# Stage 1 from six products instead of seven, its blocks evicted by ScalarE and summed by GpSimd, with side work moved to the end of a turn

## The chip, the core and the metric

The kernel runs on one core of a Trainium2 chip. The metric is device time in microseconds for one execution. The engines are TensorE (PE in the profile, with its weight loads as PEld), VectorE (DVE), ScalarE (ACT), GpSimd (POOL) and SyncE (SP), which issues nearly all DMAs. All data are fp32.

## The reference

A residual block is computed over x of shape 128 x 64 x 1024 (samples, channels, length): four one-dimensional convolutions with three taps and 64 channels, whose weights are modulated per sample by a style vector and demodulated.

```python
s = style @ mw.T + mb
weight = SCALE * w * s[:, None, :, None]
demod = lax.rsqrt(jnp.sum(weight * weight, axis=(2, 3)) + EPS)
weight = weight * demod[:, :, None, None]
...
TYPES = ('same', 'upsample', 'same', 'downsample')
...
x = x + _L0_cond_ref(x, cond_512, weights, biases, mod_w, mod_b)
```

`upsample` is a transposed convolution followed by a blur, `downsample` a blur followed by a convolution of stride two. There is no nonlinearity between the layers. So, away from the ends of a row, the four layers are for each sample one convolution of 64 x 64 matrices, and that is how the kernel treats them.

## The kernel before

The 128 samples are taken four at a time: 32 groups, numbered q. For each group the combined taps are built out of the layers' weights in three chained stages of small matmuls, and then x is convolved with them.

**Weights of a group.** `scale3(q)` (ScalarE) makes `wd`, the scaled weights of the last layer. **Stage 1** multiplies them with the third layer's weights: two kernels of three taps give one of five, the blocks S0 to S4 of 64 columns, kept in the tile S (eight slots of 64 columns for each of two row halves). From group 3 on (`DIRECT`), all but group 6 of these are computed in two parts, `stage1_a` and `stage1_b`, which work from sums of taps (`w3x`, `w2n`, made once by `split_weights`): seven products of 64 columns in five groups of matmuls. The first part leaves products in the PSUM tile psS, ScalarE evicts them with a factor `tBn`, and the second part goes on accumulating into the same PSUM; VectorE then evicts the two mixed blocks, and GpSimd makes one sum (L484). **Stage 2** (PSUM psR) convolves S with the blur E. For groups 8 to 30 two of its sums are shared: `share_sums` (VectorE) adds blocks of S, `share` multiplies them one turn ahead into spare columns of psA, and `share_copy` (ScalarE) copies them into psR as its starting values: the seeds. The evicted result is R; `r_sums` adds two more blocks to it. **Stage 3** (`stage3_b`, `stage3_a`) gives the taps Wf, and `combine_a` and `combine_b` (VectorE) make the tiles H from them.

psS, psR and psW are three uses of the same two PSUM buffers (pool `ps_w`, one buffer for each of its two tags). So the seeds of stage 2, or its first matmul where there are none, wait for the last eviction of psS.

**The convolution** is in Toom-Cook form: from the input planes X, VectorE makes G (`in_g01` and `in_g2`, at L712), and from G and X the five tiles T0 to T4 (`in3`, `in04` on VectorE; `in1`, `in2` on GpSimd, L776 and L781). Five products `conv0` to `conv4` (L803) of 340 columns go to psA, or for `conv4` to the one PSUM tile Y, which `sum2` (VectorE, two instructions) fills with starting values just before.

**Order.** Everything is issued in an order written out by hand; each engine runs its own list in that order and waits on semaphores. Groups 0 to 3 are done in `early_turn`, the middle ones in `turn_of(q)` (which works on q, n = q+1, c = q+2 and s = q+4 at once; q = 4 is called the entry), the last three in code of their own. TensorE's order in a middle turn is: stage 2 of c, `conv2(q)`, `stage3_b(c)`, `conv4(q)`, `stage3_a(c)`, `conv3(n)`, `stage1_a(s)`, `conv0(q)`, `stage1_b(s)`, `share(c+1)`, `conv1(n)`. In four turns (`SLOTS`: 10, 14, 15, 19) a further set of matmuls for the ends of the rows stands before `conv1(n)`. `SIDE` is a table by q of small work on VectorE, for those ends and for later groups: one to four short instructions in 21 turns besides the entry's own.

**Lines that matter below.** L428: matmuls of stage 1. L399: ScalarE's scaled evictions (S, R, Wf) and wd. L484: GpSimd's sum in S. L481: VectorE's eviction of stage 1. L506 and L589: matmuls of stage 2. L638: `r_sums`. L712: every multiply-add of VectorE (G, H, `sum1`, `sum2`). L761: `in3`. L790: `in04`. L803: convolutions. L880: outputs.

Of the kernel before, what the change touches and what calls it, by code (L numbers as in the profile page):

```python
# [63 lines left out]
def kernel(  # L64
# [339 lines left out]
    w3x = const.tile([P, 5, C], F32, name="w3x")  # L404
    w2n = const.tile([P, 5, C], F32, name="w2n")

    def split_weights():
        nc_g.tensor_copy(w3x[:, :K], w3)
        nc_g.tensor_scalar_mul(w2n[:, :K], woi[2], -1.0)
        for t, src in ((w3x, w3), (w2n, woi[2])):  # L410
            nc_g.tensor_add(t[:, K:], src[:, : K - 1], src[:, 1:])
# [3 lines left out]
    def scale3(q, engs=(nc_a, nc_a)):  # L415
        wd = []
        src = w3 if q < DIRECT else w3x
        n = src.shape[1]
        for j in range(2):
            t = wd_pool.tile([P, 5, C], F32, tag="wd", name=f"wd{q}_{j}")  # L420
            scaled_copy(engs[j], t[:, :n], src, tA[:, q, j : j + 1])
            wd.append(t)
        chain[q] = wd
# [17 lines left out]
    def flat(t):  # L441
        return t.rearrange("c a o -> c (a o)")
# [3 lines left out]
    def stage1(q, pool=None, engs=(nc_a, nc_a), between=None):  # L446

        wd = chain[q]
        ps = unit(pool or ps_w, f"psS{q}")
        for k, (at, at1) in enumerate(((0, 3), (3, 1), (1, 4))):  # L450
            tap_matmul(ps, wd, at, 2, woi[2][:, k, :], EVEN, first=k == 0)
            tap_matmul(ps, wd, at1, 1, woi[2][:, k, :], slice(1, 2), last=k == K - 1)
        if between:
            between()
        st, _ = s_tiles(q)
        for r in range(2):
            scaled_copy(engs[r], flat(st[r][:, 1:6]), ps[r][:, : 5 * C], tB[:, q, r : r + 1])
        chain[q] = st
        return ps

    def stage1_a(q, ps=None):

        ps = ps or unit(ps_w, f"psS{q}")
        wd = chain[q]
        tap_matmul(ps, wd, 2, 2, w2n[:, 0, :], EVEN, first=True)
        tap_matmul(ps, wd, 3, 2, w2n[:, 2, :], EVEN)
        tap_matmul(ps, wd, 1, 1, w2n[:, 1, :], slice(1, 2))
        st, t = s_tiles(q)
        for r in range(2):
            scaled_copy(nc_a, flat(st[r][:, :4]), ps[r][:, C : 5 * C], tBn[:, q, r : r + 1])  # L470
        chain[q] = wd, ps, st, t

    def stage1_b(q):

        wd, ps, st, t = chain[q]
        tap_matmul(ps, wd, 2, 1, w2n[:, 3, :], slice(3, 4))
        tap_matmul(ps, wd, 4, 1, w2n[:, 4, :], slice(4, 5), last=True)
        for r in range(2):
            p1 = st[r][:, 0:1, :].to_broadcast([P, 2, C])
            sums = ps[r][:, 2 * C : 6 * C].rearrange("c (a b o) -> c a b o", a=2, b=2)[:, :, 0]  # L480
            nc_v.scalar_tensor_tensor(  # L481
                st[r][:, 4:6, :], sums, tB[:, q, r : r + 1], p1, op0=ALU.mult, op1=ALU.subtract
            )
        nc_g.tensor_add(t[:, :, 2], t[:, :, 2], t[:, :, 0])  # L484
        chain[q] = st
        whole[q] = t
# [12 lines left out]
    def share_sums(q):  # L499
        t = whole[q]  # L500
        nc_v.tensor_add(t[:, :, 6:8], t[:, :, 1:5:3], t[:, :, 2:6:3])
# [13 lines left out]
    def share(q, ps):  # L515

        at = [NB + 4 + i * C for i in range(3)]
        p12, p34 = ([b[:, i:j] for b in ps] for i, j in zip(at, at[1:]))
        chain_matmul(p12, E[:, 2], chain[q], slice(6, 7))
        chain_matmul(p34, E[:, 6], chain[q], slice(6, 7))  # L520
        chain_matmul(p34, E[:, 5], chain[q], slice(7, 8), True)
        shared_ps[q] = [b[:, at[0] : at[2]] for b in ps]
# [12 lines left out]
    def stage2_rest(q):  # L535
# [5 lines left out]
            (apart, E[:, 0], slice(1, 4, 2)),  # L541
            (block(1), Ed[:, 0], slice(2, 3)),
            (block(2), Ed[:, 1], slice(1, 2)),
            (block(3), E[:, 2], slice(3, 4)),
            (block(3), Ed[:, 2], slice(2, 3)),
            (block(4), Ed[:, 3], slice(1, 2)),
            (block(4), E[:, 4], slice(3, 4)),
            (block(5, 2), E[:, 8], slice(2, 4)),
            (block(5), E[:, 6], slice(3, 4)),
            (block(1, 2), E[:, 1], slice(4, 6)),  # L550
            (block(2), E[:, 3], slice(4, 5)),
            (block(3), Ed[:, 4], slice(5, 6)),
            (block(4), Ed[:, 5], slice(4, 5)),
            (block(5), E[:, 7], slice(5, 6)),
# [22 lines left out]
    def stage2_taps(q, taps, ps):  # L577

        st = chain[q]
        for n in taps:  # L580
            e = n - 2
            if e % 2 == 0:
                a, lo, m = slice(1, 4), e // 2 + 1, 3
            else:
                a, lo, m = slice(4, 6), (e + 3) // 2, 2
# [897 lines left out]
    def turn_of(q):  # L1483
        n, c, s = q + 1, q + 2, q + 4
        entry = q == FIRST
        stage2(c)
        if entry:
# [33 lines left out]
        side(SIDE, q)  # L1521
# [30 lines left out]
        if s + 1 < NQ:  # L1552
            scale3(s + 1)
# [168 lines left out]
```

## Time and profile before

| what | us |
|---|---|
| median of 3 runs (lowest, highest) | 475.72 (475.56, 475.97) |
| span of the profiled execution | 475.5 |
| granted TensorE clock, mean | 0.998 |
| ScalarE busy | 312.0 |
| GpSimd busy | 165.8 |
| 28 calls of in1, of in2 on GpSimd, mean | 1.652, 1.660 |
| 31 calls of in04 on VectorE, mean | 1.585 |
| HBM traffic over the span | 145 GB/s |

The span runs from the first to the last instruction; the runs lie 0.06 to 0.47 us above it. In a row of the timeline stand the start, the time to the end of the last of the xN instructions merged in it, engine and line, what is written from what, the shape, and in brackets the idle time before it and what ended that. Two numbers after a group's bar are its busy time in us and the mean of one in ns. The start of an instruction that waits for a shared resource, not for a semaphore, is the start of its wait, so its time contains that wait. TensorE's ends are modelled; the start of the next group is the better guide to when it was done.

### The profile page before, as it was taken

What the parts mean: (1) busy time and instruction counts of PE and PEld (TensorE: products, weight loads), DVE (VectorE), ACT (ScalarE), POOL (GpSimd) and SP (SyncE); (2) the same over time, 40 slices, a digit from 0 to 9 for tenths busy, and PEclk for the clock granted to TensorE, in tenths of its full rate; (3) what the DMA queues carried; (4) which work ended last, traced back from release to release, by engine and by line L of the source; (5) the groups of instructions that cost most, each with busy time, mean ns of one, the idle gap of its engine ahead of it and who ended that gap; (6) DMA issues with size and microseconds to landing.
All of it is one profiled execution on the core that took longest, in us unless ns stands there. A gap on an engine that the chain in (4) does not pass through costs nothing.

```text
span 475.5 us, 26771 instructions
## 1 busy us (share of the span) xinstructions
PE 469.7 (99%) x11932; PEld 349.5 (74%) x11932; DVE 417.3 (88%) x694; ACT 312.0 (66%) x711; POOL 165.8 (35%) x200
## 2 busy tenths in 40 slices
PE   9999999999999999999999999999999999999996
PEld 6987788777678876677776677766788787876653
DVE  3889998879989998899979899979998999999896
ACT  4565657577766676766667666667666777766464
POOL 3634033664444342233432233422333423243200
PEclk9999999999999999999999999999999999999999
DMA  5237456535445554345544454543555544455225
GB/s 176 71 115 224 150 151 180 152 113 177 139 145 166 166 166 136 123 150 169 163 150 126 130 168 152 178 124 121 152 164 169 164 145 147 148 152 161 80 91 193
DMA packets 52707, 70.71 MB, mean 149 GB/s; under 512 B 6000, under 2 KB 50672, under 8 KB 52592
## 3 DMA queue, kind: packets, MB, share of 16 engines
q1 hardware_dynamic: 52368, 68.78, 46.3%
q8 instruction: 93, 1.52, 1.4%
q10 hardware_dynamic: 224, 0.22, 0.1%
q14 instruction: 22, 0.18, 0.1%
HBM read 35.36 MB, written 33.62 MB: 145 GB/s over the span
## 4 chain that ended last, share of the span: by engine, by line
PE 99%; DVE 0%; ACT 0%; issue 0%
PE psA L803 47%; PE Y L803 12%; PE psR L506 9%; PE psW L621 7%; PE psA L621 7%; PE psS L428 6%; PE psR L589 5%; PE psA L506 2%; PE Y L1044 2%; PE Y L183 1%; PE Y L379 1%; PE psM L220 0%; PE psE L1044 0%; PE Y L255 0%; DVE o L882 0%; PE psM L255 0%
## 5 line engine op out<-in xcount | busy, mean ns | idle before, releaser
L803 PE MATMUL psA<-T,H 64*64 64x340 f32 x2304 | 185.9, 446 | 0.0
L803 PEld LDWEIGHTS psA<-T,H 64*64 64x64 f32 x2304 | 90.7, 133 | 46.9 <-issue 2.5
L712 DVE SCALAR_TENSOR_TENSOR G<-X 128x1376 f32<-128x1376 f32 (+2 forms) x65 | 78.0, 1206 | 0.2
L776 POOL TENSOR_TENSOR T<-G 128x684 f32<-128x684 f32 x28 | 46.3, 1652 | 73.7 <-DVE G L712 73.7
L484 POOL TENSOR_TENSOR S<-S 128x128 f32<-128x128 f32 x28 | 21.6, 772 | 139.7 <-ACT S L399 139.6
L399 ACT ACTIVATE R<-psR,tC 128x448 f32<-128x448 f32 x63 | 36.6, 631 | 43.6 <-PE psR L506 25.8
L803 PE MATMUL psA<-T,Wf 64*64 64x340 f32 x768 | 63.7, 446 | 0.0
L803 PE MATMUL Y<-T,Wf 64*64 64x340 f32 x768 | 62.4, 451 | 0.0
L712 DVE SCALAR_TENSOR_TENSOR Y<-m,psA 128x340 f32<-128x340 f32 x62 | 32.0, 516 | 28.2 <-PE psA L803 26.9
L399 ACT ACTIVATE psW<-psA 128x128 f32<-128x128 f32 x100 | 19.3, 268 | 49.1 <-PE psA L621 45.0
L790 DVE TENSOR_TENSOR T<-G 128x1368 f32<-128x1368 f32 (+1 forms) x33 | 50.8, 1541 | 0.0
L399 ACT ACTIVATE Wf<-psW,t 128x256 f32<-128x256 f32 (+2 forms) x76 | 32.7, 480 | 26.7 <-PE psW L621 26.4
L761 DVE TENSOR_TENSOR T<-X 128x684 f32<-128x684 f32 x32 | 47.7, 1492 | 0.0
L506 PE MATMUL psR<-S,E 64*64 64x64 f32 (+1 forms) x1472 | 46.8, 237 | 0.0
L781 POOL TENSOR_TENSOR T<-G 128x684 f32<-128x684 f32 x28 | 46.5, 1660 | 0.0
L428 PEld LDWEIGHTS psS<-wd,w2n 64*64 64x64 f32 x1120 | 35.1, 133 | 12.9 <-issue 0.3
L506 PEld LDWEIGHTS psR<-S,E 64*64 64x64 f32 x1472 | 39.5, 134 | 4.9 <-ACT psR L529 0.2
L803 PEld LDWEIGHTS Y<-T,Wf 64*64 64x64 f32 x768 | 30.3, 132 | 16.8
L803 PEld LDWEIGHTS psA<-T,Wf 64*64 64x64 f32 x768 | 29.8, 133 | 14.5
L880 ACT ACTIVATE o<-psA,tb,td 128x340 f32<-128x340 f32 x63 | 37.1, 648 | 5.0 <-PE psA L803 2.8
L880 ACT ACTIVATE o<-y,tb,td 128x340 f32<-128x340 f32 x62 | 38.5, 678 | 0.0
L880 ACT ACTIVATE o<-Y,tb,td 128x340 f32<-128x340 f32 x62 | 36.1, 639 | 2.8 <-PE Y L803 2.0
(180 smaller groups left out, 840.4 us busy)
## 6 DMA issues: line engine op xcount, KB each, us to landing
out<-o SPq DMA_DIRECT2D x191, 170.0 KB, 2.6
X<-in_x SPq DMA_DIRECT2D x150, 172.0 KB, 3.4
X<-in_x SPq DMA_DIRECT2D x14, 516.0 KB, 5.0
par<-in_params SPq DMA_DIRECT2D x3, 192.0 KB, 3.8
Xe<-in_x_ends SPq DMA_DIRECT2D x1, 512.0 KB, 4.5
out<-Oe SPq DMA_DIRECT2D x2, 96.0 KB, 2.1
out<-o ACTq DMA_DIRECT2D x1, 170.0 KB, 2.8
par<-in_params SPq DMA_DIRECT2D x1, 160.0 KB, 2.7
```

The costliest lines, as they stand in the source:

```text
L399: nc_a.activation(dst, src, AF.Copy, scale=f)
L428: nc.tensor.matmul(ps[r][cols, at * C : (at + n) * C], weight[rows], wd[c if r == 0 else 1 - c][rows, taps], start=first, stop=last, skip_ ...
L506: nc.tensor.matmul(dst[r][cols], weight[rows], st[c if r == 0 else 1 - c][rows, slots, :], start=False, stop=last, skip_group_check=True,)
L589: nc.tensor.matmul(ps[r][cols, lo * C : (lo + m) * C], E[rows, e + 2, :], src[rows, a, :], start=(n == 0), stop=(n == 8), skip_group_check ...
L621: nc.tensor.matmul(dst[r][cols], weight[rows], t[rows, c, slots, :], start=first, stop=last, skip_group_check=True,)
L712: nc_v.scalar_tensor_tensor(out, x, f, y, op0=ALU.mult, op1=op)
L761: nc_v.tensor_sub(t[:, pairs, 0, :NJ], plane(X, 3, pairs), plane(X, 1, pairs))
L776: eng.tensor_add(t[:, :, 0, :NJ], plane(g, 2), plane(g, 1))
L781: eng.tensor_sub(t[:, :, 1, :NJ], plane(g, 2), plane(g, 1))
L790: nc_v.tensor_sub(t[:, pairs, :, :NJ], both(a, PL), both(b, 1))
L803: nc.tensor.matmul(ps[s][cols, :NB], w, Ts[q, tag][rows, c, i, g : g + NB], start=(g == 0 and (m == 3 or alone)), stop=(g == K - 1), skip_ ...
L880: nc_a.activation(dst, src, AF.Identity, bias=add, scale=d3)
```

## The change

Stage 1 of the split groups is written with six products of one block each: three in `stage1_a`, three in `stage1_b`, each group of matmuls 64 columns wide. ScalarE evicts everything: in the first part two instructions per half in place of one (two blocks into slots 0 and 4, one into slot 6), in the second one of three blocks per half, which VectorE had done. GpSimd makes S1, S2 and S3 final with four instructions in place of one (L472, L473, L484, L485 of the new file). `w3x`, `w2n` and `wd` have six blocks instead of five, so `scale3` copies 384 columns instead of 320. S0 to S4 lie in slots 0 to 4; the slot numbers in stage 2 follow. In `stage1` of groups 0, 1, 2 and 6 the same nine products are issued as three groups of 192 columns instead of six of 128 and 64.

In the middle turns `scale3(s)` moves from the end of the turn before to behind stage 2; `in_g01` follows `in_g2` directly; the seeds (`share`, `share_copy`) stand ahead of the outputs `outputs(q, 1)` and `outputs(q, 0)`; and the side work of turn q+1 is issued at the end of turn q, behind `in3` and `in1`.

```diff
-        tap_matmul(ps, wd, 2, 2, w2n[:, 0, :], EVEN, first=True)
-        tap_matmul(ps, wd, 3, 2, w2n[:, 2, :], EVEN)
-        tap_matmul(ps, wd, 1, 1, w2n[:, 1, :], slice(1, 2))
+        for n, (i, at) in enumerate(((0, 1), (2, 3), (1, 4))):
+            tap_matmul(ps, wd, at, 1, w2n[:, i, :], slice(i, i + 1), first=n == 0)
         st, t = s_tiles(q)
         for r in range(2):
-            scaled_copy(nc_a, flat(st[r][:, :4]), ps[r][:, C : 5 * C], tBn[:, q, r : r + 1])
+            src = ps[r][:, C : 5 * C].rearrange("c (a b o) -> c a b o", a=2, b=2)[:, :, 0]
+            scaled_copy(nc_a, st[r][:, 0:5:4, :], src, tBn[:, q, r : r + 1])
+            scaled_copy(nc_a, st[r][:, 6], ps[r][:, 4 * C : 5 * C], tBn[:, q, r : r + 1])
+        nc_g.tensor_add(t[:, :, 7], t[:, :, 0], t[:, :, 4])
+        nc_g.tensor_sub(t[:, :, 7], t[:, :, 7], t[:, :, 6])
...
-        tap_matmul(ps, wd, 2, 1, w2n[:, 3, :], slice(3, 4))
-        tap_matmul(ps, wd, 4, 1, w2n[:, 4, :], slice(4, 5), last=True)
+        for n, (i, at) in enumerate(((3, 1), (4, 3), (5, 2))):
+            tap_matmul(ps, wd, at, 1, w2n[:, i, :], slice(i, i + 1), last=n == K - 1)
         for r in range(2):
-            p1 = st[r][:, 0:1, :].to_broadcast([P, 2, C])
-            sums = ps[r][:, 2 * C : 6 * C].rearrange("c (a b o) -> c a b o", a=2, b=2)[:, :, 0]
-            nc_v.scalar_tensor_tensor(
-                st[r][:, 4:6, :], sums, tB[:, q, r : r + 1], p1, op0=ALU.mult, op1=ALU.subtract
-            )
-        nc_g.tensor_add(t[:, :, 2], t[:, :, 2], t[:, :, 0])
+            src = ps[r][:, C : 4 * C].rearrange("c (a o) -> c a o", o=C)
+            scaled_copy(nc_a, st[r][:, 1:4, :], src, tB[:, q, r : r + 1])
+        nc_g.tensor_sub(t[:, :, 2], t[:, :, 2], t[:, :, 7])
+        nc_g.tensor_sub(
+            t[:, :, 1:4:2], t[:, :, 1:4:2], t[:, :, 6:7].to_broadcast([P, 2, 2, C])
+        )
...
         in_g2(c)
-        side(SIDE, q)
+        in_g01(c)
+        if entry:
+            side(SIDE, q)
+        conv0(q, *((2,) if entry else range(K)))
+        if entry:
+            conv1(n, 0, 1)
+        if s < NQ:
+            stage1_b(s)
         if q in SMALL:
             l, bs = SMALL[q]
             nc_v.memset(high(bs.stop - bs.start), 0.0)
-        conv0(q, *((2,) if entry else range(K)))
-        if entry:
-            conv1(n, 0, 1)
-        outputs(q, 1)
-        if s < NQ:
-            stage1_b(s)
-        in_g01(c)
         if sharing(q):
             share(c + 1, banks(q))
             share_copy(c + 1)
+        outputs(q, 1)
         outputs(q, 0)
...
         in1(c, nc_g)
-        if s + 1 < NQ:
-            scale3(s + 1)
+        side(SIDE, q + 1)
```

Three places show how the instructions moved. The first is VectorE's list at the end of turn 12, from `in04` on: G, S and X are the tiles above, y is `sum1`, T `in3`, Y `sum2`, and Ye and g belong to side work. Before:

```order
L790 TENSOR_TENSOR T_13_3996<-G_3729 128x4x342
L501 TENSOR_TENSOR S_3721<-S_3721 128x2x128
L712 SCALAR_TENSOR_TENSOR G_3999<-X_105 128x2x342
L1066 TENSOR_TENSOR Ye_161<-Ye_161,c_156 128x64x6
L481 SCALAR_TENSOR_TENSOR S_3991<-psS_0_3977,tB,S_3991 128x128
L481 SCALAR_TENSOR_TENSOR S_3991<-psS_1_3978,tB,S_3991 128x128
L712 SCALAR_TENSOR_TENSOR G_3999<-X_105 128x2x688
L712 SCALAR_TENSOR_TENSOR y_13_4062<-psA_3884,m_13_3994 128x680
L761 TENSOR_TENSOR T_14_4064<-X_105 128x2x342
L712 SCALAR_TENSOR_TENSOR Y<-m_13_3994,psA_3884 128x340 x2
```

and with the change:

```order
L793 TENSOR_TENSOR T_13_4063<-G_3787 128x4x342
L504 TENSOR_TENSOR S_3775<-S_3775 128x2x128
L715 SCALAR_TENSOR_TENSOR G_4066<-X_105 128x2x342
L715 SCALAR_TENSOR_TENSOR G_4066<-X_105 128x2x688
L715 SCALAR_TENSOR_TENSOR y_13_4133<-psA_3947,m_13_4061 128x680
L764 TENSOR_TENSOR T_14_4135<-X_105 128x2x342
L1019 SCALAR_TENSOR_TENSOR g_159<-par,g_159 128x192 x2
L715 SCALAR_TENSOR_TENSOR Y<-m_13_4061,psA_3947 128x340 x2
```

The eviction of stage 1 has left VectorE, the two parts of G are neighbours, and the side work (here that of turn 13) stands between `in3` and `sum2`.

The second is GpSimd's list over a middle turn and the start of the next (S: sums of stage 1; T: `in1`, then `in2`; R: `r_sums`). Before:

```order
L484 TENSOR_TENSOR S_5104<-S_5104 128x2x64
L776 TENSOR_TENSOR T_18_5179<-G_5112 128x2x342
L638 TENSOR_TENSOR R_5241<-R_5241 128x2x128
L781 TENSOR_TENSOR T_18_5179<-G_5112 128x2x342
L484 TENSOR_TENSOR S_5374<-S_5374 128x2x64
```

and with the change:

```order
L472 TENSOR_TENSOR S_4334<-S_4334 128x2x64
L473 TENSOR_TENSOR S_4334<-S_4334 128x2x64
L484 TENSOR_TENSOR S_4334<-S_4334 128x2x64
L485 TENSOR_TENSOR S_4334<-S_4334 128x2x2x64
L779 TENSOR_TENSOR T_15_4419<-G_4346 128x2x342
L641 TENSOR_TENSOR R_4477<-R_4477 128x2x128
L784 TENSOR_TENSOR T_15_4419<-G_4346 128x2x342
```

Three more instructions on S stand ahead of `in1`; the first two follow ScalarE's first eviction, the last two its second.

The third is GpSimd's list in the first early turn, where S of group 3 is made (t, td and Da are small tables for later groups). Before:

```order
L335 TENSOR_TENSOR tC<-dm 64x8 x2
L934 TENSOR_TENSOR c0f<-dm,par_s 128x16
L484 TENSOR_TENSOR S_842<-S_842 128x2x64
L335 TENSOR_TENSOR t_136<-dm,var 64x8 x2
L332 TENSOR_SCALAR td<-dm 64x8 x2
L930 TENSOR_TENSOR Da<-sc,dm 128x16
```

and with the change:

```order
L335 TENSOR_TENSOR tC<-dm 64x8 x2
L937 TENSOR_TENSOR c0f<-dm,par_s 128x16
L472 TENSOR_TENSOR S_808<-S_808 128x2x64
L473 TENSOR_TENSOR S_808<-S_808 128x2x64
L484 TENSOR_TENSOR S_808<-S_808 128x2x64
L485 TENSOR_TENSOR S_808<-S_808 128x2x2x64
L335 TENSOR_TENSOR t_136<-dm,var 64x8 x2
L332 TENSOR_SCALAR td<-dm 64x8 x2
```

S of group 3 is read by stage 2 at the start of the next early turn. Its even taps read S0, S2 and S4, its odd taps S1 and S3; they follow GpSimd's third and fourth instruction where they followed ScalarE's and VectorE's evictions and GpSimd's one sum.

More of the change, by code (lines that the diff above doesn't have):

```diff
@@ L401, in scaled_copy @@
             eng.tensor_scalar(dst, src, f, None, op0=ALU.mult)
-    w3x = const.tile([P, 5, C], F32, name="w3x")
-    w2n = const.tile([P, 5, C], F32, name="w2n")
+    w3x = const.tile([P, 6, C], F32, name="w3x")
+    w2n = const.tile([P, 6, C], F32, name="w2n")
     def split_weights():
@@ L449, in stage1 @@
         ps = unit(pool or ps_w, f"psS{q}")
-        for k, (at, at1) in enumerate(((0, 3), (3, 1), (1, 4))):
-            tap_matmul(ps, wd, at, 2, woi[2][:, k, :], EVEN, first=k == 0)
-            tap_matmul(ps, wd, at1, 1, woi[2][:, k, :], slice(1, 2), last=k == K - 1)
+        for k in range(K):
+            tap_matmul(ps, wd, k, K, woi[2][:, k, :], slice(0, K), first=k == 0, last=k == K - 1)
         if between:
@@ L518, in share @@
         p12, p34 = ([b[:, i:j] for b in ps] for i, j in zip(at, at[1:]))
-        chain_matmul(p12, E[:, 2], chain[q], slice(6, 7))
-        chain_matmul(p34, E[:, 6], chain[q], slice(6, 7))
-        chain_matmul(p34, E[:, 5], chain[q], slice(7, 8), True)
+        chain_matmul(p12, E[:, 2], chain[q], slice(5, 6))
+        chain_matmul(p34, E[:, 6], chain[q], slice(5, 6))
+        chain_matmul(p34, E[:, 5], chain[q], slice(6, 7), True)
         shared_ps[q] = [b[:, at[0] : at[2]] for b in ps]
@@ L1486, in turn_of @@
         stage2(c)
+        if s < NQ and not entry:
+            scale3(s)
         if entry:
```

37 lines of the change are left out of this document (19 added, 18 removed).

## The prediction

> **What bounds the kernel now.** I read the busy line and the chain of waits of the page first, then the timeline of one middle turn (turn 12) engine by engine.
>
> ```profile
> PE 469.7 (99%) x11932; PEld 349.5 (74%) x11932; DVE 417.3 (88%) x694; ACT 312.0 (66%) x711; POOL 165.8 (35%) x200
> PE 99%; DVE 0%; ACT 0%; issue 0%
> 215.10 0.40 PE L506 MATMUL psR<-S,E 64*64 64x128 f32 x8
> 228.94 0.40 PE L506 MATMUL psR<-S,E 64*64 64x128 f32 x8
> ```
>
> TensorE is the bound. A middle turn, from one stage 2 to the next, is 228.94 − 215.10 = 13.84 us of matmuls without gaps. So work taken from TensorE is gained in full, and any new wait of TensorE is lost in full. There is one place where such a wait is very near:
>
> ```profile
> 204.91 0.94 PE L621 MATMUL psA<-R,w0s 64*64 64x192 f32 x24
> 206.28 1.95 PE L803 MATMUL Y<-T,Wf 64*64 64x340 f32 x24
> 205.16 1.07 DVE L712 SCALAR_TENSOR_TENSOR Y<-m,psA 128x340 f32<-128x340 f32 x2 [0.97 <-PE psA L803]
> ```
>
> conv2 ends where stage3_b begins (204.91), `sum2` starts 0.25 later, ends at 206.23, and conv4 starts 0.05 behind it. Stage3_b covers this chain with nothing to spare. VectorE came to `sum2` 0.97 us early; whatever uses up more than that stops TensorE.
>
> **Saved on TensorE.** Groups of matmuls start one behind the other, so starts give the price.
>
> ```profile
> 210.53 0.73 PE L428 MATMUL psS<-wd,w2n 64*64 64x128 f32 x24
> 211.08 1.90 PE L803 MATMUL psA<-T,Wf 64*64 64x340 f32 x24
> 212.80 0.41 PE L428 MATMUL psS<-wd,w2n 64*64 64x64 f32 x16
> 213.03 0.53 PE L506 MATMUL psA<-S,E 64*64 64x64 f32 x24
> ```
>
> Stage 1 takes 211.08 − 210.53 = 0.55 and 213.03 − 212.80 = 0.23, together 0.78. Two groups of eight at 64 columns take 0.23, so one takes 0.115. Six of them: 0.69, or 0.68 with 0.114. Saved: 0.10 per split group; GpSimd's sum L484 stands once in each, and there are 28 (row below). **−2.8 us.** The direct groups issue the same columns in fewer instructions: nothing taken, up to −0.2.
>
> **The price of the sums: VectorE and GpSimd share something.** GpSimd's single sum has very different durations for one shape:
>
> ```profile
> L484 POOL TENSOR_TENSOR S<-S x28: 455/821/1622, 40.6 to 426.5; 128x128 f32<-128x128 f32 x28
> 142.56 1.58 DVE L712 SCALAR_TENSOR_TENSOR G<-X 128x1376 f32<-128x1376 f32 x1
> 142.83 1.62 POOL L484 TENSOR_TENSOR S<-S 128x128 f32<-128x128 f32 x1
> 215.42 0.87 DVE L712 SCALAR_TENSOR_TENSOR y<-psA,m 128x680 f32<-128x680 f32 x1
> 215.64 1.65 POOL L776 TENSOR_TENSOR T<-G 128x684 f32<-128x684 f32 x1 [2.61 <-DVE G L712]
> 216.21 1.81 DVE L761 TENSOR_TENSOR T<-X 128x684 f32<-128x684 f32 x1
> ```
>
> The 0.455 us sum, begun under VectorE's G, ended at 144.45, 0.31 after G's end at 144.14. The other way round, `in3`, begun under `in1`, ended at 218.02, 0.73 after `in1` (217.29). So two such instructions exclude each other from start to end; who holds it first finishes, the waiting one goes next and then needs about 0.14 less than its own duration. `sum1` (y), which reads PSUM, ran beside `in1` in its usual 0.87. By the Trainium skill ("SBUF — State Buffer", section "Who interferes with whom") the shared ports are an exclusive lock in which issue order decides who blocks, and a VectorE instruction with at most one SBUF input stays out of it; these rows agree. The change removes a VectorE eviction that read PSUM, and adds three GpSimd sums that read SBUF in each of the 28 groups.
>
> **The first turns,** where S is read by the very next stage 2.
>
> ```profile
> 41.34 1.61 DVE L790 TENSOR_TENSOR T<-G 128x1368 f32<-128x1368 f32 x1
> 43.39 1.58 DVE L712 SCALAR_TENSOR_TENSOR G<-X 128x1376 f32<-128x1376 f32 x1
> 43.35 2.91 PE L589 MATMUL psR<-S,E 64*64 64x192 f32 x72
> 54.52 1.23 ACT L880 ACTIVATE o<-y,tb,td 128x340 f32<-128x340 f32 x2
> 55.83 1.58 DVE L712 SCALAR_TENSOR_TENSOR G<-X 128x1376 f32<-128x1376 f32 x1
> 57.82 2.72 PE L589 MATMUL psR<-S,E 64*64 64x192 f32 x70
> 71.45 0.58 ACT L270 ACTIVATE var<-Y,eps 128x384 f32<-128x384 f32 x1
> 73.18 2.72 PE L589 MATMUL psR<-S,E 64*64 64x192 f32 x72
> 99.47 1.17 ACT L880 ACTIVATE o<-Y,tb,td 128x340 f32<-128x340 f32 x2
> 101.21 2.71 PE L589 MATMUL psR<-S,E 64*64 64x192 f32 x70
> 204.72 0.73 POOL L638 TENSOR_TENSOR R<-R 128x256 f32<-128x256 f32 x1 [1.27 <-ACT R L399]
> 211.86 0.87 DVE L712 SCALAR_TENSOR_TENSOR G<-X 128x684 f32<-128x684 f32 x1
> L399 ACT ACTIVATE Wf<-psW,t 128x192 f32<-128x192 f32 x13 | 4.8, 419 | 0.6 <-PE psW L621 0.5 <-PE Y L964 0.2
> ```
>
> Prices: the third sum (128 elements) 0.46, the fourth (256, like `r_sums`) 0.73, behind a lock 0.3 and 0.6; ScalarE's second eviction is two of 192 elements, 0.42 each, about 0.73 with overlapping starts. Stage 2's first tap, eight matmuls, takes 2.72 × 8/70 = 0.31; then the odd tap needs the fourth sum. Stage 2 itself could start 0.1 earlier than now.
> - Turn 0: `in04` holds the third sum until 42.95, so it ends at 43.3. VectorE, without its 0.60 eviction, has reached G by then and holds the lock to 44.75; fourth sum to 45.35. The odd tap, due at 43.56, starts about 45.45: 1.9, of which 0.2 is there already (2.91 against 2.72). +1.7.
> - Turn 1: evictions end about 56.45 (outputs to 55.75, then 0.73), G holds the lock to 57.41, third sum to 57.72, `in_g2` (0.87) to 58.46, fourth sum to 59.06; due 58.03. +1.1 with the tap's start.
> - Turn 2: ScalarE is in its queue until 72.03, evictions to 72.8, sums to 73.3 and 74.1; due 73.39. +0.7.
> - Turn 4: the outputs end at 99.47 + 0.2 (a later start) + 1.17 = 100.8, evictions at 101.5; due 101.1. +0.4.
>
> Sum **+3.9**; with the lock free each time only ScalarE's lateness is left, 0.7 + 0.4 = 1.1; with one more VectorE instruction ahead of each fourth sum it is 5.
>
> **The middle turns: ScalarE.**
>
> ```profile
> 211.29 0.84 ACT L399 ACTIVATE S<-psS,tBn 128x256 f32<-128x256 f32 x2 [0.32 <-PE psS L428]
> L399 ACT ACTIVATE S<-psS,tBn 128x256 f32<-128x256 f32 x56 | 23.5, 471 | 11.6 <-PE psS L428 11.6
> 213.80 0.63 ACT L529 COPY psR<-psA 128x256 f32<-128x256 f32 x2
> 217.33 1.16 ACT L399 ACTIVATE R<-psR,tC 128x448 f32<-128x448 f32 x2 [0.91 <-POOL T L776]
> ```
>
> 192 elements cost 419 ns and 256 cost 471, so 64 cost 52: 128 elements 0.37, 64 some 0.32. First evictions: 2 × (0.37 + 0.32) less 0.3 of overlap, 1.06, begun at 211.08 (0.21 earlier than now, the first part being shorter) and done at 212.14, or 212.45 without overlap; stage1_b needs them at 212.60. Second evictions 213.16 to 213.9, seeds (0.63) to 214.6, against stage 2 at 215.02. All hidden: 0. The two outputs behind them, 1.2 each, end about 216.8, before R's eviction (217.33). The moved `scale3` lies behind R's eviction in ScalarE's idle time there. By the Trainium skill ("ScalarE: Activation LUTs", section "Rules for kernel authors": about 0.3 us per ACTIVATE plus 0.83 ns per element) the four first evictions would be 2 × (0.41 + 0.35) = 1.52, done at 212.60, and stage1_b could be up to 0.1 late in each of some 25 turns, 2.5 us more; but the same rule makes 256 elements 0.51, where the trace has 0.471 and overlapping starts.
>
> **The middle turns: GpSimd, `in3`, side work.**
>
> ```profile
> 212.21 0.82 POOL L484 TENSOR_TENSOR S<-S 128x128 f32<-128x128 f32 x1 [5.16 <-ACT S L399]
> 213.90 1.58 DVE L712 SCALAR_TENSOR_TENSOR G<-X 128x1376 f32<-128x1376 f32 x1
> 212.64 0.81 DVE L1066 TENSOR_TENSOR Ye<-Ye,c 128x384 f32<-128x384 f32 x1
> 231.98 0.74 DVE L1016 SCALAR_TENSOR_TENSOR g<-par,g 128x192 f32<-128x192 f32 x2
> ```
>
> `in_g2` (211.86) holds the first sum until 212.73, and it ends at 213.03, as the one sum does now; `in_g01` follows at once and holds the lock to 214.47; second sum 214.8, third 215.3, fourth 216.0, `in1` to 217.6. `sum1` waits for conv1 as before, so `in3` queues about 216.1, is held until 217.6 and ends at 218.35 (218.02 before). `sum2` is due 0.25 after conv2, 218.93. So side work, which stood at 212.64 at no cost, has 0.58 us. One instruction of 0.5 to 0.67 fits within some hundredths: 0. But `r_sums` asks for the lock when R's eviction is done, 217.33 + 1.16 = 218.49, and where side work has several instructions it comes between them: 218.35 + 0.74 + 0.6 − 0.26 = 219.43, `sum2` 0.5 late. The side work of turn q + 1 now stands at the end of turn q; at the end of turns 10, 14, 15 and 19 the extra matmuls give it time. Of the other turns, six have several side instructions (those of turns 5, 6, 7, 10, 13 and 18), and that of 13 has two such sets: 7 × 0.5 = **+3.5**, bounds 0 (`in3` as early as now, `r_sums` behind the side work) and 7 (each set behind two locks).
>
> **Sum:** −2.8 + 3.9 + 3.5 = +4.6. Against the profiled execution (span 475.5, with 0.2 around it 475.7, as the median 475.72): **480.3 us.**
>
> **The rivals.**
> - *B, the sums find the lock free* (faster): GpSimd's first two sums slip in ahead of `in_g2`, the fourth follows the third before VectorE asks, `in3` stays at 218.02. Speaks for it: the first part of stage 1 ends 0.21 sooner, so the first sum asks sooner. Against: L484's median is 821 ns against 455 alone, so it is usually held today. 475.7 − 2.8 + 1.1 = 474.0. What decides is which engine asks first, at 42.95 and at 212.0.
> - *C, `r_sums` goes ahead of the single side instructions too* (much slower): `in3` ends at 218.35 and `r_sums` asks at 218.49, a margin of 0.14. If it is lost in all 11 turns with one instruction, 11 × 0.6 = 6.6 more: 486.9.
> - *D, only the first turns pay*: side work fits, 475.7 − 2.8 + 3.9 = 476.8.
> - *E, ScalarE's evictions run without overlap and stage1_b waits* 0.1 in 25 turns: 482.8.
>
> **How the numbers follow.** Main case 0.36, B 0.28, D 0.18, C 0.13, E 0.05. A measurement of this kernel can tell 0.2%, 0.95 us, from no change. B is faster; D lies at +1.1, on the edge, so half of it is "same"; a few hundredths go to faster and to same from a main case with smaller terms. Faster 0.30, same 0.12, slower 0.58. The main case alone, between its bounds, reaches from 476.8 (side work at 0) to 484.9 (5 and 7); with B below, less 0.6 for its own parts, and C above, plus 0.6, the range is 473.4 to 487.5.
>
> **What would show it.** Right: stage 2 of turns 0 and 1 lasting 3.8 us and more in place of 2.7 to 2.9; middle turns without side work at 13.74; those with several side instructions 0.3 to 0.5 above that, with TensorE waiting for `sum2` ahead of conv4; L484's successors at L472 and L473 often far over 455 ns. Wrong: TensorE waiting for psS at stage1_b or for the seeds, turns all alike at 13.74, or first turns as short as before.

## The result: 2.65% slower, and the profile after

| | before | changed |
|---|---|---|
| median of 6 runs, us (lowest, highest) | 476.52 (475.56, 477.39) | 489.48 (487.2, 490.25) |
| ratio of times, 95% interval | | 1.0265 (1.0241 to 1.0288) |
| span of the profiled execution, us | 475.5 | 488.0 |

The forecast was 480.3 us, +4.6, with a range to 487.5: the direction was right, but the medians lie 13.0 us apart, nearly three times as much. The run that was profiled took 489.91 us, 1.9 above its span. So the 0.2 us that the prediction set between a span and a run was wrong too (it compared one execution's span with other executions' times), but it stands on both sides of the difference: the spans are 12.5 us apart.

The page of the changed kernel, its busy line and its chain of waits (after the engine, busy us, share of the span and number of instructions; then shares of the chain):

```profile
PE 473.1 (97%) x12060; PEld 346.5 (71%) x12060; DVE 423.4 (87%) x638; ACT 339.4 (70%) x823; POOL 261.2 (54%) x286
PE 88%; DVE 7%; ACT 2%; POOL 2%; issue 1%; DVEq 0%; POOLq 0%
```

The chain was 99% TensorE; now 12% of it runs through other engines. TensorE's waits in the changed kernel (who waits, for whom, us in all, times, longest):

```profile
PE Y L806 <- DVE Y L715: 4.0, 3, 2.2
PE psR L592 <- POOL S L485: 1.5, 1, 1.5
PE psA L806 <- POOL S L473: 1.5, 1, 1.5
PE psA L624 <- POOL R L641: 0.4, 1, 0.4
```

The first row is conv4 waiting for `sum2`. Waits under 0.15 us don't show here, so the account below goes by the starts of stage 2, which both timelines have for every group; the difference of two starts is a turn, and the difference between the kernels is what the turn lost.

| where | changed minus before, us |
|---|---|
| up to the first turn's stage 2 (the start varies by 2 us between profiles of any of these kernels) | −1.0 |
| turns 0 to 4, the early ones and the entry | +5.2 |
| turns 7, 10 and 18, with several side instructions | +6.7 (0.8, 1.95, 3.99) |
| turns 11 and 13 to 17 | +1.8 |
| the other middle turns, −0.2 to +0.2 each | −0.1 |
| sum before rounding, equal to 488.0 − 475.5 | 12.5 |

Turns 5 to 28 are the middle ones; together they lost 8.4. Turn 10 shows how it goes. VectorE and GpSimd in the changed kernel (start, duration, engine, line, what is written from what):

```profile
177.51 0.86 DVE L764 TENSOR_TENSOR T<-X 128x684 f32<-128x684 f32 x1
178.29 1.67 DVE L1028 TENSOR_TENSOR a<-dm 64x64 f32<-64x64 f32 x1
179.88 0.18 DVE L1029 COPY c<-c0f 64x64 f32<-64x64 f32 x1
180.07 0.66 DVE L1028 TENSOR_TENSOR a<-dm 64x64 f32<-64x64 f32 x1
180.66 1.63 DVE L1029 COPY c<-c0f 64x64 f32<-64x64 f32 x1
182.32 1.07 DVE L715 SCALAR_TENSOR_TENSOR Y<-m,psA 128x340 f32<-128x340 f32 x2
...
177.56 2.32 POOL L779 TENSOR_TENSOR T<-G 128x684 f32<-128x684 f32 x1
179.88 0.78 POOL L641 TENSOR_TENSOR R<-R 128x256 f32<-128x256 f32 x1
180.61 1.63 POOL L784 TENSOR_TENSOR T<-G 128x684 f32<-128x684 f32 x1
...
183.44 0.80 PE L806 MATMUL Y<-T,Wf 64*64 64x340 f32 x8 [1.47 <-DVE Y L715]
```

`in3` (L764) asks at 177.51, `in1` (L779) at 177.56. So `in3` goes first and takes 0.86; `in1` waits for it and ends at 179.88. The side work's first instruction, a table of 64 x 64 that takes 0.20 alone, waits for all of `in1` (1.67). Then `r_sums` (L641) gets between, then `in2` (L784), for which the last side instruction waits 1.63. `sum2` starts at 182.32, some 2 us late, and conv4 with it. The groups of the whole run tell of the same change of places: `in3` and `in1`, before and after (busy us, mean ns of one):

```profile
L761 DVE TENSOR_TENSOR T<-X 128x684 f32<-128x684 f32 x32 | 47.7, 1492 | 0.0
L776 POOL TENSOR_TENSOR T<-G 128x684 f32<-128x684 f32 x28 | 46.3, 1652 | 73.7 <-DVE G L712 73.7
```

```profile
L764 DVE TENSOR_TENSOR T<-X 128x684 f32<-128x684 f32 x32 | 36.8, 1151 | 0.0
L779 POOL TENSOR_TENSOR T<-G 128x684 f32<-128x684 f32 x28 | 54.2, 1934 | 7.2 <-DVE G L715 7.2
```

Before, `in3` was the one that waited (0.86 alone, 1.49 on average) and `in1` never did. Now `in3` waits less and `in1` more, which frees VectorE earlier, for side work that then runs against `in1`, `r_sums` and `in2` one after the other.

### The profile page after: what moved, and what is told of

It is laid out like the page before. It is cut to its first block, busy times and chain, and to the rows that moved or that the text cites. A ratio compares the mean times of both kernels' runs of the same rounds, so it can differ in the third digit from the quotient of the medians.

```text
span 488.0 us, 27215 instructions
## 1 busy us (share of the span) xinstructions
PE 473.1 (97%) x12060; PEld 346.5 (71%) x12060; DVE 423.4 (87%) x638; ACT 339.4 (70%) x823; POOL 261.2 (54%) x286
## 4 chain that ended last, share of the span: by engine, by line
PE 88%; DVE 7%; ACT 2%; POOL 2%; issue 1%; DVEq 0%; POOLq 0%
PE psA L806 42%; PE Y L806 11%; PE psR L509 8%; PE psW L624 7%; PE psA L624 5%; PE psS L429 5%; PE psR L592 4%; PE psA L509 2%; PE Y L1047 2%; DVE Y L715 1%; DVE T L764 1%; ACT S L399 1%; DVE H L715 1%; DVE g L1019 1%; POOL S L485 1%
## 5 line engine op out<-in xcount | busy, mean ns | idle before, releaser
L472 POOL TENSOR_TENSOR S<-S 128x128 f32<-128x128 f32 x28 | 27.8, 993 | 138.1 <-ACT S L399 138.1
L715 DVE SCALAR_TENSOR_TENSOR G<-X 128x1376 f32<-128x1376 f32 (+2 forms) x65 | 82.3, 1304 | 0.2
L806 PE MATMUL Y<-T,Wf 64*64 64x340 f32 x768 | 63.6, 460 | 4.1 <-DVE Y L715 4.0
L779 POOL TENSOR_TENSOR T<-G 128x684 f32<-128x684 f32 x28 | 54.2, 1934 | 7.2 <-DVE G L715 7.2
L715 DVE SCALAR_TENSOR_TENSOR y<-psA,m 128x680 f32<-128x680 f32 x31 | 26.9, 866 | 23.7 <-PE psA L806 22.4
L784 POOL TENSOR_TENSOR T<-G 128x684 f32<-128x684 f32 x28 | 47.3, 1688 | 0.0
L806 PEld LDWEIGHTS Y<-T,Wf 64*64 64x64 f32 x768 | 29.1, 134 | 23.6 <-DVE Y L715 5.4
L715 DVE SCALAR_TENSOR_TENSOR H<-Wf 128x384 f32<-128x384 f32 x64 | 42.4, 662 | 0.0
L429 PEld LDWEIGHTS psS<-wd,w2n 64*64 64x64 f32 x1344 | 32.8, 134 | 12.3
L473 POOL TENSOR_TENSOR S<-S 128x128 f32<-128x128 f32 x28 | 39.9, 1423 | 2.2
```

Of the source, the lines that this page charges most:

```text
L429: nc.tensor.matmul(ps[r][cols, at * C : (at + n) * C], weight[rows], wd[c if r == 0 else 1 - c][rows, taps], start=first, stop=last, skip_ ...
L472: nc_g.tensor_add(t[:, :, 7], t[:, :, 0], t[:, :, 4])
L473: nc_g.tensor_sub(t[:, :, 7], t[:, :, 7], t[:, :, 6])
L715: nc_v.scalar_tensor_tensor(out, x, f, y, op0=ALU.mult, op1=op)
L779: eng.tensor_add(t[:, :, 0, :NJ], plane(g, 2), plane(g, 1))
L784: eng.tensor_sub(t[:, :, 1, :NJ], plane(g, 2), plane(g, 1))
```

## Experiments

All are compared with the kernel before, run beside them. Times are medians; "ratio" is against the kernel before, with its 95% interval. Losses of a turn are again differences between starts of stage 2.

**1. The changed kernel, side work back in its old place.**

```diff
         in_g2(c)
+        side(SIDE, q)
         in_g01(c)
-        if entry:
-            side(SIDE, q)
...
-        side(SIDE, q + 1)
```

> The changed kernel with the side work of the middle turns back in its old place, between in_g2 and in_g01; all else as changed. Theory 1 (the side work at the turn's end, cut up by r_sums and in2 on GpSimd, is the largest cost): TensorE's waits for sum2 in turns 7, 10 to 16 and 18 go, about 9 us, and the half-speed stretch of turn 18 with them; 479 to 481 us. Rival (the three added sums make in1, in3 and in2 late, and the side work only shows it): 485 us or more, with waits for sum2 or r_sums left in the middle turns.

483.26 us, ratio 1.0149 (1.0118 to 1.0179), between the two. Turn 10 loses 0.02 in place of 1.95, turn 18 0.06 in place of 3.99, and the sum over the middle turns falls from 8.4 to 0.5. What is left is the 5.2 of the first turns. Theory 1 has the place right, and its size was too high: 7.9 us by the starts of stage 2 and 6.2 by the medians, where 9 were expected.

**2. The kernel before, with its side work alone moved to the turn's end.**

```diff
-        side(SIDE, q)
+        if entry:
+            side(SIDE, q)
...
+        side(SIDE, q + 1)
```

> The kernel before with only its side work moved to the end of the turn before (behind in3 and in1), old stage 1 and old order otherwise. Theory 1: the collisions with r_sums and in2 come there too, with the old stage 1: 5 to 9 us slower than before, sum2 late by 1.5 to 2.5 us in turns 10 and 18. Rival (the added sums are needed for the loss): in3 ends 0.33 us earlier and the side work fits, 0 to 1.5 us slower.

478.9 us, ratio 1.0064 (1.0042 to 1.0087). A miss for theory 1: the move alone costs 2.5 us, not 5 to 9. Turn 18 loses 2.1 and turn 7 0.4, all others nothing, turn 10 among them:

```profile
172.01 1.65 POOL L776 TENSOR_TENSOR T<-G 128x684 f32<-128x684 f32 x1 [2.58 <-DVE G L712]
174.97 0.73 POOL L638 TENSOR_TENSOR R<-R 128x256 f32<-128x256 f32 x1 [1.31 <-ACT R L399]
...
172.61 1.78 DVE L761 TENSOR_TENSOR T<-X 128x684 f32<-128x684 f32 x1
174.31 0.20 DVE L1025 TENSOR_TENSOR a<-dm 64x64 f32<-64x64 f32 x1
174.78 0.19 DVE L1026 COPY c<-c0f 64x64 f32<-64x64 f32 x1
```

Here `in1` asks 0.6 before `in3` and goes first; when the side work starts at 174.31, GpSimd is idle until `r_sums` at 174.97, and four instructions pass in 0.66 us. The same four took 4.0 us in the changed kernel. So in turn 10 neither the move nor the sums alone make the loss, but the two together. Turn 18 is different: there the move alone makes 2.1 of the 3.99, and its four instructions take 2.95 us, held by `r_sums` and `in2`. The 2.5 us lie outside both expectations, nearer to the rival's 1.5. Theory 2, which runs 5 and 6 try: what decides is whether `in1` or `in3` asks first. In the changed kernel the fourth sum ends 1.2 us after the start of stage 2 at the end of twelve of the turns 5 to 27 and 1.0 at the end of five (earlier in the others, most of them with extra matmuls), and `in3` is asked for at 1.1. (Why it is the one or the other was not followed further.)

**3. First turns by the direct stage 1** (groups 3, 4, 5 and 7: nine products, no sums on GpSimd).

```diff
-            stage1_a(s)
+            stage1(s)
...
-            stage1_b(s)
```

> The changed kernel with groups 3, 4, 5 and 7 by the direct stage 1 (nine products, ScalarE's eviction, no sums on GpSimd), as group 6 already is. Theory (the waits of the first turns come from the sums, through the lock with VectorE and through late in1 and in2): stage 2 of turns 0 to 2 back to 2.6 to 2.75 us, no wait of 1.5 us in turn 3; 4 to 5 us gained less 4 x 0.3 for the longer products, so 485 to 486 us. Rival (ScalarE's queue is what is late): under 1.5 us gained.

485.37 us, ratio 1.0191 (1.0159 to 1.0222): 4 us under the changed kernel. Turns 0 to 4 lose 1.5 in place of 5.2, some 0.8 of which is the longer stage 1 itself (0.98 us in place of 0.78 in each of four groups). So the sums, and what they make late, are most of what the first turns lost.

**4. The four side instructions of turn 18 in two turns.**

```diff
-        18: lambda: (rest1_edges(0), rest1_edges(1)),
+        18: lambda: rest1_edges(0),
+        19: lambda: rest1_edges(1),
```

> The changed kernel with the four side instructions of turn 18 in two turns, two for turn 18 and two for turn 19. Theory (each instruction behind the first waits for one GpSimd instruction; and the idle time of 2.25 us is what takes the granted clock to 0.60 for the next 3.4 us): TensorE waits 0.5 us or less for sum2 in turn 18 and in turn 19, the clock stays at 1.00, 2.5 to 3.5 us less than the changed kernel. Rival (the clock falls for another reason, and the waits only move): 0 to 1 us less.

487.62 us, ratio 1.0237 (1.0212 to 1.0263). Turn 18 loses nothing (−0.07 in place of 3.99) and turn 19 0.27; the clock stays at 1.00 there. 2.6 us less by span, about 1.9 by medians, where 2.5 to 3.5 were expected (another turn, 11, lost 0.5 more in the profiled execution).

**5. The same instructions, `in1` ahead of the last two sums.**

```diff
-            stage1_b(s)
+            stage1_b(s, False)
...
         in1(c, nc_g)
+        if s < NQ:
+            last_sums(s)
```

> The changed kernel with the same instructions, but in the middle turns GpSimd's in1 stands ahead of its last two sums on S, not behind them. Theory 2 (what costs in the middle turns is which engine asks first: with the fourth sum ending 1.2 us after the start of stage 2 and in3 asked for at 1.1, in3 goes ahead of in1, in1 ends 1.2 us later, and the side work's instructions then wait for in1, r_sums and in2): with in1 first the 2.0 us of turn 10 go, the 0.15 us at stage 3 in the late turns go, turns 13 to 16 lose under 0.2 each; turn 18 keeps 2 us or more, since its four instructions meet r_sums and in2 in any case; 485 to 486.5 us. Rival (the number of sums is what costs, not their place): within 0.7 us of the changed kernel.

482.1 us, ratio 1.0129 (1.0087 to 1.017), 7 us under the changed kernel and better than theory 2 said. No instruction was added or taken away; only GpSimd's order differs. Turn 10 loses 0.32 and turn 18 0.39:

```profile
176.93 1.09 POOL L491 TENSOR_TENSOR S<-S 128x128 f32<-128x128 f32 x1
177.98 0.73 POOL L492 TENSOR_TENSOR S<-S 128x256 f32<-128x256 f32 x1
178.86 0.73 POOL L646 TENSOR_TENSOR R<-R 128x256 f32<-128x256 f32 x1 [0.15 <-ACT R L399]
...
177.63 0.47 DVE L1033 TENSOR_TENSOR a<-dm 64x64 f32<-64x64 f32 x1
178.03 0.73 DVE L1034 COPY c<-c0f 64x64 f32<-64x64 f32 x1
178.77 0.22 DVE L1033 TENSOR_TENSOR a<-dm 64x64 f32<-64x64 f32 x1
178.91 0.74 DVE L1034 COPY c<-c0f 64x64 f32<-64x64 f32 x1
```

The side work still meets one GpSimd instruction after the other, but these are two sums and `r_sums`, of 0.46 to 0.73 us alone, where they were `in1` and `in2` of 1.65 with `r_sums` between: 2.0 us for the four, not 4.0. My "turn 18 keeps 2 us or more" was a miss for the same reason. The number of sums is not what costs in the middle turns; the length of what the side work runs into is.

**6 to 8. S1 and S3 made by VectorE straight from PSUM** (so that the fourth sum goes), with the side work at the turn's end (6), back between the two parts of G (7), or behind G (8). In all three VectorE's eviction stands behind `in_g01`.

```diff
-            src = ps[r][:, C : 4 * C].rearrange("c (a o) -> c a o", o=C)
-            scaled_copy(nc_a, st[r][:, 1:4, :], src, tB[:, q, r : r + 1])
+            scaled_copy(nc_a, st[r][:, 2], ps[r][:, 2 * C : 3 * C], tB[:, q, r : r + 1])
+            src = ps[r][:, C : 5 * C].rearrange("c (a b o) -> c a b o", a=2, b=2)[:, :, 0]
+            nc_v.scalar_tensor_tensor(
+                st[r][:, 1:4:2, :],
+                src,
+                tB[:, q, r : r + 1],
+                st[r][:, 6:7, :].to_broadcast([P, 2, C]),
+                op0=ALU.mult,
+                op1=ALU.subtract,
+            )
         nc_g.tensor_sub(t[:, :, 2], t[:, :, 2], t[:, :, 7])
-        nc_g.tensor_sub(
-            t[:, :, 1:4:2], t[:, :, 1:4:2], t[:, :, 6:7].to_broadcast([P, 2, 2, C])
-        )
```

> The changed kernel with S1 and S3 made by VectorE straight from PSUM (one SBUF operand, as the old stage 1 did), ScalarE evicting S2 alone in the second part, and GpSimd's fourth sum gone. Theory 2: in1 starts about 0.1 us after the start of stage 2, always ahead of in3; turn 10 loses nothing, turn 18 still 2 us or more; the odd tap of the first turns waits 0.3 us or less in place of 1.6, 0.4 and 0.4, and turn 3 under 0.5 in place of 1.5; 479 to 482 us. Rival (VectorE's time is what is short, and 0.6 us more of it per turn is lost again): 486 us or more.

484.86 us, ratio 1.0175 (1.0148 to 1.0201). Half right. Turns 1 and 2 lose nothing now (−0.3 together, in place of 2.4), and turns 10 and 18 lose 0.2 and 0.6; turn 3's wait stays (1.3, where under 0.5 was expected). But nearly every middle turn now loses 0.2 to 0.4, which neither theory had.

> As the run with S1 and S3 on VectorE, and the side work back between in_g2 and in_g01. If the two causes add up: the first turns cost 1 us or less, no wait of TensorE over 0.3 us in the middle turns, stage 1 saves 0.09 us in each split group: 474.5 to 477 us, level with the kernel before or up to 1.5 us under it. Rival: VectorE, with side work, both parts of G and the eviction in a row, is late for sum1 and so for sum2 in the turns with side work, 0.3 to 0.5 us in 15 turns: 480 us or more.

499.8 us, ratio 1.049 (1.0458 to 1.0521). A clear miss, and the waits of this kernel name the cause:

```profile
PE psR L514 <- ACT psR L537: 15.0, 17, 1.6
```

Stage 2 waits for its seeds, in 17 turns. The seeds go into a PSUM buffer that psS holds until VectorE has evicted it; with G and the side work ahead of that eviction it is about 1 us late. Run 6 has the same wait in a small form: some 0.2 us ahead of most stage 2s and 0.15 in them.

> As the run before, but the side work behind in_g01, so that G is whole before it. in1 then starts before the side work ends: in1 0.5 us earlier than in the run before, TensorE's time the same within 0.5 us, unless the side work, now against in1, is held by it for 1.6 us and sum1 is late (then 3 us or more slower than the run before).

506.29 us, ratio 1.0624 (1.0596 to 1.0652), by the same wait (17.9 us in 18 turns, up to 3.0): the side work, now against `in1`, stands ahead of the eviction as well. It is the "unless" of the expectation, at more than twice its 3 us.

**9 and 10. As run 7, with the eviction ahead of `in_g01` again** (as in the kernel before), then with the direct stage 1 in the first turns. The cuts of the diff are against the changed kernel.

```diff
         in_g2(c)
-        in_g01(c)
-        if entry:
-            side(SIDE, q)
+        side(SIDE, q)
...
             stage1_b(s)
...
+        in_g01(c)
...
-        side(SIDE, q + 1)
```

> As the run with S1 and S3 on VectorE and the side work back, with in_g01 behind VectorE's eviction of stage 1 again. Theory (the 15 us that the two runs with the eviction behind in_g01 lost stand at the seeds, which wait for the last eviction of psS): the seeds are in time, TensorE's waits at stage 2 of the middle turns go, the first turns cost 2 us and stage 1 saves 0.09 in some 23 turns: 475.5 to 478 us. Rival (VectorE is simply overfull with side work and eviction): 485 us or more.

> As the run before with groups 3, 4, 5 and 7 by the direct stage 1 as well. If first and middle turns add up: the first turns cost 1.3 us in place of 2.3, so 1 us under the run before: 474.5 to 477 us. Rival: no difference between the two.

476.83 us, ratio 1.0013 (0.9996 to 1.003), and 476.7 us, ratio 1.003 (1.0014 to 1.0046). The 15 us at the seeds are gone, as the theory of run 9 said; VectorE was not overfull. The two don't differ, so the rival of run 10 held: its first turns cost 1.5 us where run 9's cost 1.4.

**11. Side work back and first turns direct, the sums as in the changed kernel.**

> The changed kernel with the side work back in its old place and groups 3, 4, 5 and 7 direct, nothing on VectorE. The two runs that did one of these each lay 6 and 4 us under the changed kernel; if they add up, 478 to 480.5 us, with TensorE's waits gone but for the turns behind the extra matmuls. Rival (both remove the same waits): 482 us or more.

478.17 us, ratio 1.0049 (1.0026 to 1.0073). The two parts add up, and a little more: 6.2 and 4.1 us under the changed kernel each alone, 11.3 together. With these two undone, what is left of the change costs 0.5%.

**12. The changed kernel once more.**

> The changed kernel once more, for its profile. If the idle time of 2.25 us in turn 18 takes the granted clock down, the stretch at 0.60 behind it is there again and turn 18 takes 17.8 us; if not, the wait is there and the clock stays at 1.00, and the turn takes 16.2 us.

489.23 us (one run). Its losses are the same turn by turn (turn 18: 17.84 us in place of 17.83), half clock included, but for turns 11 and 16, which lost 0.2 and 0.4 less; so what those lost is not firm. It also bears on theory 2: at the start of turn 18 `in3` went first here and `in1` in the first profile, and the turn took the same time. More of both below.

**13 and 14. As run 9, with the old seven products for groups 3, 4, 5 and 7; then also the second half of turn 13's side work moved into turn 14.**

```diff
+        if q < 8:
+            tap_matmul(ps, wd, 2, 2, w2n[:, 0, :], EVEN, first=True)
+            tap_matmul(ps, wd, 3, 2, w2n[:, 2, :], EVEN)
+            tap_matmul(ps, wd, 1, 1, w2n[:, 1, :], slice(1, 2))
...
+        14: lambda: setup1(1),
...
-    LATE = {13: lambda: setup1(1)}
+    LATE = {}
```

> As the run with S1 and S3 on VectorE in the old order, but groups 3, 4, 5 and 7 by the old seven products (VectorE for S1 and S3, one GpSimd sum), so that the first turns are as before. If the saving of stage 1 is real time and only waits ate it: the first turns cost 0.3 us or less in place of 1.2, the middle turns 13.76 in place of 13.84; 0.5 to 1.5 us under the kernel before, 474.3 to 475.5 us. Rival (the 0.09 us come back in other matmuls of each turn): level with the kernel before or above.

> As the run before, with the second half of turn 13's side work (until now behind in3 at that turn's end) at the side work's place in turn 14. If it is this that cost 0.42 us ahead of conv4 in turn 14 in the last runs: 0.4 us under the run before, 474.0 to 475.0 us. Rival: no difference.

475.37 us, ratio 0.999 (0.9974 to 1.0007), and 475.25 us, ratio 0.9995 (0.998 to 1.001). The saving is there in the timeline; a middle turn of run 13, by two starts of stage 2:

```profile
386.05 0.40 PE L542 MATMUL psR<-S,E 64*64 64x128 f32 x8
399.81 0.40 PE L542 MATMUL psR<-S,E 64*64 64x128 f32 x8
```

13.76 us, where a turn without waits took 13.84 before, and from the first turn on the two profiles gain 0.9 us by the starts of stage 2. In the times this is lost in their spread (473.97 to 476.51 us, and 474.25 to 477.3 of the kernel before), so no version here is shown to beat the kernel before. Taking the late work out of turn 13 moved some 0.4 us of loss from conv4 to the extra matmuls of turn 14, so the rival of run 14 held. Runs 9, 13 and 14 keep the other moves of the change (`scale3`, the seeds ahead of the outputs) and are level with the kernel before: those moves cost nothing that these runs can tell.

## Why the prediction was wrong, point by point

- **Saving on TensorE, −2.8.** Right in kind, a little high: stage 1 takes 0.70 in place of 0.78 by the starts behind it, so some 0.08 in each of 28 groups, 2.2, where 0.10 was taken. It is seen as time where the waits are gone (run 13).
- **The shared lock.** Right. It is the mechanism of most of what was lost: the second sum (L473), 0.46 alone, takes 1.42 on average. The sentence on the one SBUF input leaves out a condition; the last section has it.
- **First turns, +3.9.** The late sums cost stage 2 nearly what was forecast. Up to the convolution behind it, it was later by 1.6 (the wait of 1.48 at its odd tap), 1.0 (0.60 ahead of it, 0.4 in it), 0.4 and 0, where 1.7, 1.1, 0.7 and 0.4 were forecast:

```profile
42.03 1.73 DVE L715 SCALAR_TENSOR_TENSOR G<-X 128x1376 f32<-128x1376 f32 x1
42.28 2.07 POOL L485 TENSOR_TENSOR S<-S 128x256 f32<-128x256 f32 x1
44.40 2.40 PE L592 MATMUL psR<-S,E 64*64 64x128 f32 x64 [1.48 <-POOL S L485]
59.07 3.09 PE L592 MATMUL psR<-S,E 64*64 64x192 f32 x72 [0.60 <-POOL S L484]
```

  That is 3.0, not 3.9; but these turns lost 5.2, mainly since I followed the late sums only to stage 2. They also make `in1` and `in2` late, and these then hold VectorE:

```profile
76.75 1.98 POOL L784 TENSOR_TENSOR T<-G 128x684 f32<-128x684 f32 x1
77.14 1.92 DVE L712 SCALAR_TENSOR_TENSOR Wf<-idn,t,Wf 128x64 f32<-128x64 f32 x2
88.67 0.86 DVE L715 SCALAR_TENSOR_TENSOR y<-psA,m 128x680 f32<-128x680 f32 x1
89.67 0.80 PE L806 MATMUL psA<-T,H 64*64 64x340 f32 x8 [1.45 <-POOL S L473]
```

  The pair at L712 takes 0.47 where nothing holds it. VectorE stays behind, `sum1` ends at 89.53, and only then is psA free for conv2, 1.45 us late in turn 3. (The profile names the sum L473, which ended at about the same time; in run 6 the same wait is put down to `sum1`, 1.3 us, and conv2 starts 0.14 to 0.15 behind `sum1` in both.) In the entry turn stage 3 waits another 0.39 for `r_sums`, which stands on VectorE there.
- **ScalarE in the middle turns, 0.** Right: the four first evictions take 1.04 us in turn 12 (1.06 forecast), and no wait for them appears there, so the rival of evictions without overlap (E) fell. Its wait of 0.1 us did not follow from its own numbers either: done at 212.45 without overlap, needed at 212.60.
- **GpSimd, `in3` and side work, +3.5: the step that failed.** The middle turns lost 8.4 us net of the saving; 0.7 was forecast for all of them (−2.8 + 3.5). The term that failed is the price of a set of several side instructions, 0.5 us a turn. It let one instruction, `r_sums`, come between them. But `in2` stands right behind `r_sums` in GpSimd's list, and it is ready; so it comes between too, and the next side instruction waits for all of it. Turn 18 shows it in the branch that the prediction had worked out, with `in1` first and `in3` ending 3.34 us after the start of stage 2 (3.33 forecast, 218.35 − 215.02); L1105 is its side work:

```profile
297.02 1.65 POOL L779 TENSOR_TENSOR T<-G 128x684 f32<-128x684 f32 x1
299.53 0.73 POOL L641 TENSOR_TENSOR R<-R 128x256 f32<-128x256 f32 x1 [0.86 <-ACT R L399]
300.23 1.68 POOL L784 TENSOR_TENSOR T<-G 128x684 f32<-128x684 f32 x1
...
299.32 2.99 DVE L1105 SCALAR_TENSOR_TENSOR Ue<-b1s,Ue 64x64 f32<-64x64 f32 x4
```

  The four take 0.26, 0.80, 1.61 and 0.27 us: the second waits for `r_sums`, the third for `in2` until 301.91. They end at 302.31, and conv4 waits 2.25 us. In run 12 `in3` went first, and the four waited for `in1` as well:

```profile
296.67 2.32 POOL L779 TENSOR_TENSOR T<-G 128x684 f32<-128x684 f32 x1
297.39 4.38 DVE L1105 SCALAR_TENSOR_TENSOR Ue<-b1s,Ue 64x64 f32<-64x64 f32 x4
```

  They end behind `in2` again, 6.27 us after the start of stage 2 (6.25 above), and conv4 waits 2.23. So which of `in1` and `in3` goes first does not decide what this turn loses, as theory 2 had it; that `in2` comes in between does. By turns, the sets cost 1.95 in turn 10, some 2.3 in turn 18, 0.8 and 0.4 in turns 7 and 13 and nothing in 5 and 6, each net of the saving. (In turn 7 half of it is another wait: stage 3 waits 0.41 for `r_sums`, which stands behind a GpSimd part of the side work.) The rest of turn 18, 1.7 us, is the clock's, for which the sum had no term; see the last section. The branch was wrong too in most turns: the prediction has the fourth sum end 1.0 us after the start of stage 2 and `in3` ask at 1.1, a margin of 0.1 us, and the sum mostly ended at 1.2. In the turns where `in3` went first for that reason and only one side instruction stood behind it, it cost under 0.2, net of the saving.
- **"Turns 10, 14, 15 and 19 have time".** Not borne out in full: the turns behind three of them (11, 15 and 16) lost 0.49, 0.17 and 0.33, in run 12 0.32, 0.11 and nothing.
- **The rivals.** B and D fell with the lock. C, `r_sums` ahead of the side work in all turns, has the time nearest to the measured one (486.9), but not its place: turns with a single side instruction lost under 0.2 outside turns 11 to 17. That it is near is luck.

## What to carry to other kernels

Where two engines exclude each other, ask for every pair which one asks first and by how much; with a margin of 0.1 us it went either way in two profiles of one kernel, so both sides have to be worked out, to the end of the queue. The cost of a short instruction in such a place is not its own length but that of the instruction that it runs into, once for each instruction as long as the other engine has one ready. And a move whose cover looks free (side work, an eviction) has to be checked against what is queued behind it: here the seeds behind VectorE's eviction cost 15 us in one run.

## What the runs showed of the hardware

**The clock after a wait.** Turn 18 lost 3.99 us in the changed kernel and 2.32 in run 3, with the same wait; the 1.7 us between them were lost behind the wait. The granted clock there, in the changed kernel (window, its length, busy time and instructions of PE, PEld, DVE, ACT and POOL, then the clock, DMA share and GB/s):

```profile
303.00:304.00 1.00, 0.53 (x8) 0.38 (x12) 0.97 (x2) 0.00 (x0) 0.00 (x0) 0.89 0.27 74
304.00:305.00 1.00, 1.00 (x16) 0.40 (x12) 1.00 (x4) 0.00 (x0) 0.00 (x0) 0.50 0.87 228
305.00:306.00 1.00, 1.00 (x12) 0.49 (x8) 0.96 (x3) 0.00 (x0) 0.00 (x0) 0.50 0.37 134
306.00:307.00 1.00, 1.00 (x16) 0.61 (x12) 0.93 (x3) 0.00 (x0) 0.00 (x0) 0.50 0.00 0
307.00:308.00 1.00, 1.00 (x39) 0.87 (x35) 1.00 (x2) 0.04 (x1) 0.00 (x0) 0.91 0.00 0
```

TensorE stood still for 2.25 us, started again at 303.47 and from about 303.8 on ran at half clock for 3.4 us (three full windows, 0.22 of the first and 0.18 of the last; the 0.60 in the expectations of runs 4 and 12 is the mean from 303 to 307). The 24 matmuls of conv4 took 3.2 us in place of 1.77. Run 12 shows it again behind an idle time of 2.23, and run 8 behind one of 3.04, each for about 3.4 us and from 0.7 us after the restart. Run 3 has the same wait of 2.24 us in the same place, with the clock at 1.00 throughout:

```profile
300.51 1.95 PE L806 MATMUL Y<-T,Wf 64*64 64x340 f32 x24 [2.24 <-DVE Y L715]
```

So the length of the idle time alone does not settle it, and the expectation of run 4 (that it does) can't be held. The Trainium skill ("TensorE: Matmul & The Clock Gate", section "What's actually happening") describes a free-running window of about 3.4 us: after an idle one the clock is halved, after a busy one it is restored. The length of the stretch fits it, and two outcomes for one wait could come of where in the window the wait falls; but 2.25 us without a matmul are less than an idle window, and they were enough here. That the place in the window decides was not tried.

**A copy waits too.** The prediction has it, without a condition, that a VectorE instruction with at most one SBUF input stays out of the lock. In turn 10 the copy at L1029, with one, took 1.63 us under `in2` and 0.19 in run 2. The Trainium skill ("SBUF — State Buffer", section "Who interferes with whom") states this only for instructions outside the faster modes that use both ports, and a copy can enter such a mode; these two rows agree with the page, and not with the sentence of the prediction.
